# A holographic stage worked off by batch, with query magnitudes inverted on GpSimd

## The chip, the core and the metric

The kernel runs on one core of one Trainium2 chip, as one launch. The metric is the device time of the execution in microseconds, the median of several runs. Beside it there is one profiled execution, whose span runs from the first to the last instruction. In what follows TensorE (PE) does matmuls and transposes, VectorE (DVE), ScalarE (ACT) and GpSimd (POOL) do element work, and SyncE (SP) issues most DMAs.

## What is computed

The reference is a perceiver of two layers on x with 2 batches of 256 tokens of 256 numbers. Each layer has a cross-attention to a context of 4096 tokens, a second attention and a feed-forward part, each added to x. The change lies in the second layer, between its cross-attention and its expert layer, in the "holographic" attention:

```python
    def _L1_attn_ref(x, Wq, bq, Wk, bk, Wv, bv):
        EPS = 1e-08

        def unit_projection(x):
            f = jnp.fft.fft(x)
            f = f / (jnp.abs(f) + EPS)
            return jnp.fft.ifft(f).real

        def bind(a, b):
            return jnp.fft.ifft(jnp.fft.fft(a) * jnp.fft.fft(b)).real

        def unbind(s, a):
            return jnp.fft.ifft(jnp.fft.fft(s) * jnp.conj(jnp.fft.fft(a))).real
        query = unit_projection(jnp.einsum('bsd,ed->bse', x, Wq) + bq)
        keys = unit_projection(jnp.einsum('bsd,ed->bse', x, Wk) + bk)
        values = unit_projection(jnp.einsum('bsd,ed->bse', x, Wv) + bv)
        x_k = bind(keys, values)
        s = jnp.cumsum(x_k, axis=1)
        out = unbind(s, query)
        return out
    ...
    x = x + _L1_xattn_ref(ctx_1024, ctx_1024, _layernorm(x, axis=-1), mask_1x1xSxS2_ik0, L1_xattn_w_out, L1_xattn_b_out)
    x = x + _L1_attn_ref(_layernorm(x, axis=-1), L1_attn_Wq, L1_attn_bq, L1_attn_Wk, L1_attn_bk, L1_attn_Wv, L1_attn_bv)
    x = x + _L1_ffn_ref(_layernorm(x, axis=-1), L1_ffn_sim_matrix, L1_ffn_gates, L1_ffn_q_proj, L1_ffn_k_proj, L1_ffn_v_proj, L1_ffn_o_proj)
```

Queries, keys and values are projections of the normalized x whose every frequency is divided by its magnitude plus 1e-8. Keys and values are multiplied frequency by frequency, summed up along the tokens, and multiplied by the conjugate of the queries.

## The kernel before, in words

Tokens lie on the 128 partitions: 4 token tiles (NT), two to a batch, so that x is a tile of 128 x 4 x 256. A program with a scheduler (the order of each engine's instructions is the scheduler's, except where `keep_in_program_order` fixes it) writes the stages one behind the other.

The second layer's cross-attention (`few_keys` or `any_mask`, one of two branches of the program) leaves its result in `xn`. Behind the branch the tokens are turned by `transpose_tokens`: TensorE transposes into two PSUM tiles, one for each half (k) of the 256 features and all four token tiles, and `evac` copies them to `xnT`, one by VectorE (L44) and one by ScalarE (L46). The output projection (L1515) takes 16 matmul records, and VectorE adds each token tile to x (L1518). Then `layernorm_T(es1, "e")` takes the statistics of all four token tiles (L119, L120), one root of 128 x 4 on ScalarE (L134), its reciprocal (L137), the normalized `xn` (L147), the transposes (L163) and the two copies to `xnT`.

The discrete Fourier transform is folded into the projections (`wq` holds weight times transform, `BD` and `pick` the bias), so `spectrum(j, b)` gives the spectrum of query, key or value (j = 0, 1, 2) of batch b directly: real parts of the frequencies 0 to 128 (NR = 129) and imaginary parts of 1 to 127, two token tiles side by side in one PSUM tile `pf`. From there:

- `keys_values(b, fk, fv)` copies the key spectrum to `ks` and squares both on ScalarE, multiplies the two spectra on VectorE (`product_real`, `product_imag`), takes the magnitudes (`magnitudes`: squares added, root on ScalarE), adds 1e-8 (L1590), multiplies the two magnitudes (L1592), takes the reciprocal on VectorE (L1593), and scales the product `xk` with it (L1594, L1595). The small operations that can be on either engine (`eng`) run on VectorE for batch 0 and on GpSimd for batch 1.
- `query_magnitudes` squares on ScalarE (L1600), adds and adds 1e-8 on GpSimd (L1602); `query_units` takes the reciprocal (L1607) and scales the query spectrum (L1608, L1609) on VectorE.
- `running_sum(b)` sums `xk` along the tokens with three matmuls by `upper` and `ones` (L1614 to L1616). The sum does not go on from one batch to the next.
- `back(b, pc, qn)` multiplies by the conjugate of the queries on VectorE (tile `z`), transposes (L1628), copies (L1630), transforms back (L1634), adds to x (L1639) and takes the statistics for the next layer normalization.

The order in which these are called is:

```python
        kv0 = spectrum(1, 0), spectrum(2, 0)
        keys_values(0, *kv0)
        kv1 = spectrum(1, 1), spectrum(2, 1)
        q0_ = spectrum(0, 0)
        mag0 = query_magnitudes(q0_)
        keys_values(1, *kv1)
        pc0 = running_sum(0)
        q1_ = spectrum(0, 1)
        mag1 = query_magnitudes(q1_)
        qn0 = query_units(q0_, mag0)
        ...
        pc1 = running_sum(1)
        back(0, pc0, qn0)
        qn1 = query_units(q1_, mag1)
        ...
        back(1, pc1, qn1)
```

The expert layer follows: `normalized(b)`, `turned(b)` (L1711, L1714), `expert_weights(b)`, and the projections L1755 in an order that is fixed. TensorE's part of it starts once batch 1 has been through `back`.

Of the kernel before, what the change touches and what calls it, by code (L numbers as in the profile page):

```python
# [9 lines left out]
F32 = mybir.dt.float32  # L10
# [3 lines left out]
ALU = mybir.AluOpType  # L14
# [3 lines left out]
P = 128  # L18
# [8 lines left out]
def tile_perceiver(ctx: ExitStack, tc: tile.TileContext, t):  # L27
    nc = tc.nc

    def pool(es, name, bufs, space=None):  # L30
        kw = {} if space is None else {"space": space}
        return es.enter_context(tc.tile_pool(name=name, bufs=bufs, **kw))
# [84 lines left out]
    def layernorm_stats(mv, sm, tt):  # L117
        st = sm.tile([P, 6], F32, name="st", bufs=2)
        nc.vector.bn_stats(st, x[:, tt, :])  # L119
        nc.vector.bn_aggr(mv[:, tt, :], st)  # L120
# [1384 lines left out]
    with cmp.Else():  # L1505
        any_mask()

    with ExitStack() as es:
        p_s = pool(es, "xo_t", 2, PSUM)
        p_e = pool(es, "xo", 4, PSUM)  # L1510
        transpose_tokens(p_s, xnT, ao)
        for tt in range(NT):
            po = p_e.tile([P, D], F32, name="pe")
            for k in range(2):
                nc.tensor.matmul(  # L1515
                    po, lhsT=xnT[:, k, tt * P : (tt + 1) * P], rhs=wo[:, k, :], start=(k == 0), stop=(k == 1)
                )
            nc.vector.tensor_add(x[:, tt, :], po, x[:, tt, :])  # L1518

    xa.close()  # L1520
    until_xattn.close()
# [6 lines left out]
    with ExitStack() as es:  # L1528
        wk = pool(es, "ha", 1)
        wk2 = pool(es, "ha2", 2)  # L1530
        oproj = wl.tile([P, 8, D], F32, name="oproj")
        nc.sync.dma_start(oproj, t["L1_ffn_o_proj"].rearrange("e d c -> (e d) c").rearrange("(j p) c -> p j c", p=P))

        with ExitStack() as es1:
            layernorm_T(es1, "e")
        ps = pool(es, "ha_p", 6, PSUM)
        ps2 = pool(es, "ha_c", 2, PSUM)
        NR = D // 2 + 1

        def spectrum(j, b):  # L1540

            pf = ps.tile([P, 2, D], F32, name="pf")
            for tb in range(2):
                tt = 2 * b + tb
                for k in range(2):
                    nc.tensor.matmul(  # L1546
                        pf[:, tb, :], lhsT=xnT[:, k, tt * P : (tt + 1) * P], rhs=wq[:, j, k, :],
                        start=(k == 0), stop=False,
                    )
                nc.tensor.matmul(pf[:, tb, :], lhsT=pick[:, j, :], rhs=BD, start=False, stop=True)  # L1550
            return pf

        def magnitudes(eng, sq, tag):

            n = sq.shape[1]
            eng.tensor_tensor(sq[:, :, 1 : NR - 1], sq[:, :, 1 : NR - 1], sq[:, :, NR:D], ALU.add)
            mag = wk2.tile([P, n, NR], F32, name=f"mag{tag}")
            nc.scalar.activation(mag, sq[:, :, 0:NR], AF.Sqrt)
            return mag

        def product_real(out, tmp, a, b_, conj):

            nc.vector.tensor_mul(out[:, :, 0:NR], a[:, :, 0:NR], b_[:, :, 0:NR])
            nc.vector.tensor_mul(tmp, a[:, :, NR:D], b_[:, :, NR:D])
            orr = out[:, :, 1 : NR - 1]
            nc.vector.tensor_tensor(orr, orr, tmp, ALU.add if conj else ALU.subtract)

        def product_imag(out, tmp, a, b_, conj):
            oi = out[:, :, NR:D]
            nc.vector.tensor_mul(oi, a[:, :, NR:D], b_[:, :, 1 : NR - 1])  # L1570
            nc.vector.tensor_mul(tmp, a[:, :, 1 : NR - 1], b_[:, :, NR:D])
            nc.vector.tensor_tensor(oi, oi, tmp, ALU.subtract if conj else ALU.add)

        xks = {}

        def keys_values(b, fk, fv):

            eng = nc.gpsimd if b else nc.vector
            ks = wk2.tile([P, 2, D], F32, name="ks")
            nc.scalar.copy(ks, fk)  # L1580
            sq = wk2.tile([P, 4, D], F32, name="sqkv")
            nc.scalar.activation(sq[:, 0:2, :], fk, AF.Square)
            nc.scalar.activation(sq[:, 2:4, :], fv, AF.Square)
            xk = wk2.tile([P, 2, D], F32, name="xk")
            tmp = wk2.tile([P, 2, NR - 2], F32, name="tmp")
            product_real(xk, tmp, fv, ks, False)
            mag = magnitudes(eng, sq, "kv")
            tmp = wk2.tile([P, 2, NR - 2], F32, name="tmp")
            product_imag(xk, tmp, fv, ks, False)
            eng.tensor_scalar_add(mag, mag, 1e-8)  # L1590
            den = mag[:, 0:2, :]
            eng.tensor_tensor(den, den, mag[:, 2:4, :], ALU.mult)  # L1592
            nc.vector.reciprocal(den, den)  # L1593
            nc.vector.tensor_mul(xk[:, :, 0:NR], xk[:, :, 0:NR], den)  # L1594
            nc.vector.tensor_mul(xk[:, :, NR:D], xk[:, :, NR:D], den[:, :, 1 : NR - 1])  # L1595
            xks[b] = xk

        def query_magnitudes(fq):
            sq = wk2.tile([P, 2, D], F32, name="sqq")
            nc.scalar.activation(sq, fq, AF.Square)  # L1600
            mag = magnitudes(nc.gpsimd, sq, "q")
            nc.gpsimd.tensor_scalar_add(mag, mag, 1e-8)  # L1602
            return mag

        def query_units(fq, mag):
            qn = wk2.tile([P, 2, D], F32, name="qn")
            nc.vector.reciprocal(mag, mag)  # L1607
            nc.vector.tensor_mul(qn[:, :, 0:NR], fq[:, :, 0:NR], mag)  # L1608
            nc.vector.tensor_mul(qn[:, :, NR:D], fq[:, :, NR:D], mag[:, :, 1 : NR - 1])  # L1609
            return qn  # L1610

        def running_sum(b):
            pc = ps2.tile([P, 2, D], F32, name="pc")
            nc.tensor.matmul(pc[:, 0, :], lhsT=upper, rhs=xks[b][:, 0, :], start=True, stop=True)  # L1614
            nc.tensor.matmul(pc[:, 1, :], lhsT=ones, rhs=xks[b][:, 0, :], start=True, stop=False)
            nc.tensor.matmul(pc[:, 1, :], lhsT=upper, rhs=xks[b][:, 1, :], start=False, stop=True)  # L1616
            return pc

        def back(b, pc, qn):
            z = wk2.tile([P, 2, D], F32, name="z")  # L1620
            tmp = wk2.tile([P, 2, NR - 2], F32, name="tmp")
            product_real(z, tmp, pc, qn, True)
            tmp = wk2.tile([P, 2, NR - 2], F32, name="tmp")
            product_imag(z, tmp, pc, qn, True)
            pt = ps.tile([P, 2, S], F32, name="pf")
            for k in range(2):
                for tb in range(2):
                    nc.tensor.transpose(pt[:, k, tb * P : (tb + 1) * P], z[:, tb, k * P : (k + 1) * P], ident)  # L1628
            zT = wk2.tile([P, 2, S], F32, name="zT")
            nc.scalar.copy(zT, pt)  # L1630
            po = ps.tile([P, 2, D], F32, name="pf")
            for tb in range(2):
                for k in range(2):
                    nc.tensor.matmul(  # L1634
                        po[:, tb, :], lhsT=zT[:, k, tb * P : (tb + 1) * P], rhs=idft[:, k, :],
                        start=(k == 0), stop=(k == 1),
                    )
            xb = x[:, 2 * b : 2 * b + 2, :]
            nc.vector.tensor_add(xb, po, xb)  # L1639
            for tt in (2 * b, 2 * b + 1):  # L1640
                layernorm_stats(mvf, wk, tt)

        kv0 = spectrum(1, 0), spectrum(2, 0)
        keys_values(0, *kv0)
        kv1 = spectrum(1, 1), spectrum(2, 1)
        q0_ = spectrum(0, 0)
        mag0 = query_magnitudes(q0_)
        keys_values(1, *kv1)
        pc0 = running_sum(0)
        q1_ = spectrum(0, 1)  # L1650
        mag1 = query_magnitudes(q1_)
        qn0 = query_units(q0_, mag0)

        sims = wl.tile([P, 2, 16], F32, name="sims")
        nc.vector.tensor_mul(sims, sim, sim)
        pc1 = running_sum(1)
        back(0, pc0, qn0)
        qn1 = query_units(q1_, mag1)
        pg = ps.tile([P, 2, D], F32, name="pf")
        for k in range(2):  # L1660
            nc.tensor.matmul(pg[:, 0, 0:16], lhsT=ones, rhs=sims[:, k, :], start=(k == 0), stop=(k == 1))
        rs = wl.tile([P, 16], F32, name="rs")
        nc.scalar.activation(rs, pg[:, 0, 0:16], AF.Sqrt)
        back(1, pc1, qn1)
        nc.vector.tensor_scalar_max(rs, rs, 1e-12)
        nc.vector.reciprocal(rs, rs)
        nc.vector.tensor_mul(sims, sim, rs.unsqueeze(1).to_broadcast([P, 2, 16]))
# [285 lines left out]
```

## Time and profile before

| | |
|---|---|
| median of 3 runs | 585.91 us (582.93 to 587.59) |
| the profiled execution | 581.55 us, of it 579.5 us span |
| TensorE busy | 519.3 us (90%), mean granted clock 0.941 |
| VectorE, ScalarE, GpSimd busy | 259.9, 184.0, 110.0 us |
| output projection, first matmul | 464.52 us |
| first matmul of the spectra | 474.70 us |
| batch 0, then batch 1 added to x (L1639) | 504.32 and 508.48 us |

Times within the span are counted from its start. The stage that the change touches is thus the stretch from some 457 to 509 us of 579.5. The times of the rows are start and duration of instructions; an idle time in brackets is that of the engine just before the instruction, with what ended it.

### The profile page before, as it was taken

The numbers are of one execution on the slowest core, as the hardware profiler recorded it, in microseconds if no ns is written. First come the engines' busy times: TensorE is split into PE (matmuls) and PEld (weight loads), VectorE is DVE, ScalarE is ACT, GpSimd is POOL, SyncE is SP. The second block draws the span as 40 slices with busy tenths as digits, with TensorE's granted clock in tenths as the row PEclk, the third lists the DMA queues.
The fourth block names the chain that finished last, engine by engine and source line by source line (L and its number), as shares of the span: only waits on it lengthen the run. The fifth ranks groups of instructions, "written<-read, shape, count | busy, mean of one in ns | idle before, by whom it ended". The sixth has DMA issues, their size and how long they took to land.

```text
span 579.5 us, 8233 instructions
## 1 busy us (share of the span) xinstructions
PE 519.3 (90%) x3083; PEld 341.6 (59%) x3083; DVE 259.9 (45%) x571; ACT 184.0 (32%) x386; POOL 110.0 (19%) x168
## 2 busy tenths in 40 slices
PE   3999999999896979999994889999999568689997
PEld 3888888883554656666662345444444356444466
DVE  4022241025465531212126757777771047767473
ACT  2211111152565202221222146666666304120110
POOL 8610100105540021100015000000000004016830
PEclk9999999999898799999998679999999779589999
DMA  8999987920002357977822000000000200002301
GB/s 300 327 309 269 276 248 194 164 45 1 1 2 69 115 189 250 298 266 257 303 84 84 1 2 2 2 1 1 3 1 1 78 1 1 1 0 62 86 1 37
DMA packets 53505, 62.73 MB, mean 108 GB/s; under 512 B 16180, under 2 KB 44188, under 8 KB 53452
## 3 DMA queue, kind: packets, MB, share of 16 engines
q1 hardware_dynamic: 45172, 51.76, 30.4%
q10 hardware_dynamic: 6504, 6.18, 3.9%
q0 software_dynamic: 1776, 4.12, 2.2%
q8 instruction: 28, 0.46, 0.3%
q14 instruction: 25, 0.20, 0.1%
HBM read 58.98 MB, written 3.07 MB: 107 GB/s over the span
## 4 chain that ended last, share of the span: by engine, by line
PE 52%; DVE 4%; issue 3%; ACT 2%; POOL 1%; DVEq 0%; SPq 0%; ACTq 0%
PE pe L1020 8%; PE pp L1755 7%; PE pav L1101 6%; PE pm L1003 6%; PE py L732 5%; PE ga L707 4%; PE ua L707 3%; PE pa L1854 2%; PE gb L707 2%; PE pT L721 2%; PE pf L1546 2%; DVE mx L1009 1%; PE pf L1634 1%; ACT e L1027 1%; PE pe L1515 1%
## 5 line engine op out<-in xcount | busy, mean ns | idle before, releaser
L1009 DVE TENSOR_REDUCE mx<-pm 128x2 f32<-128x1024 f32 x64 | 77.9, 1223 | 31.7 <-PE pm L1003 31.5
L1027 ACT ACTIVATE e<-pe 128x512 f32<-128x512 f32 x128 | 72.7, 597 | 43.9 <-PE pe L1020 38.5
L1020 PE MATMUL pe<-qe,both 32*128 32x256 f32 x512 | 76.3, 412 | 2.0 <-DVE mx L1009 1.4
L1003 PE MATMUL pm<-both 32*128 32x512 f32 x256 | 74.4, 710 | 0.9 <-DVE both L990 0.9
L1020 PEld LDWEIGHTS pe<-qe,both 32*128 32x128 f32 x512 | 45.9, 190 | 32.7 <-SPq L1084 24.5
L394 PE MATMUL ph<-xnT,ct 128*128 128x256 f32 x256 | 61.9, 387 | 1.5 <-ACT xnT L46 1.5
L368 PE MATMUL acc<-cn,g 128*128 128x256 f32 x256 | 60.6, 380 | 0.4 <-ACT g L399 0.4
L394 PEld LDWEIGHTS ph<-xnT,ct 128*128 128x128 f32 x256 | 49.6, 195 | 8.7 <-ACT xnT L46 1.9
L368 PEld LDWEIGHTS acc<-cn,g 128*128 128x128 f32 x256 | 48.5, 190 | 8.0 <-ACT g L399 1.2
L399 ACT ACTIVATE g<-ph 128x512 f32<-128x512 f32 x32 | 19.1, 597 | 91.9 <-PE ph L394 63.7
L1755 PE MATMUL pp<-proj,xnT 128*128 128x512 f32 x96 | 44.7, 615 | 0.0
L1101 PE MATMUL pav<-e,both 128*32 128x256 f32 x512 | 40.5, 391 | 0.0
L732 PE MATMUL py<-wd,hT 128*128 128x256 f32 x156 | 38.6, 389 | 1.4 <-ACT hT L723 1.4
L732 PEld LDWEIGHTS py<-wd,hT 128*128 128x128 f32 x156 | 27.9, 189 | 10.5 <-issue 5.6
L331 DVE TENSOR_SCALAR is<-mi 128x512 f32<-128x512 int32 x16 | 6.8, 426 | 58.2 <-DMA mi<-in_maskT 58.2
L1770 POOL TENSOR_TENSOR pw<-pw 128x512 f32<-128x512 f32 (+2 forms) x30 | 25.0, 832 | 38.3 <-DVE pw L1760 36.7
L1755 PEld LDWEIGHTS pp<-proj,xnT 128*128 128x128 f32 x96 | 18.1, 196 | 20.1 <-issue 20.1
L1677 POOL MEMSET causal<- 128x512 f32 x1 | 0.5, 524 | 131.5 <-PE pav L1101 131.5
L1003 PEld LDWEIGHTS pm<-both 32*128 32x128 f32 x256 | 20.2, 203 | 3.7 <-issue 1.7
L1101 PEld LDWEIGHTS pav<-e,both 128*32 128x32 f32 x512 | 10.4, 108 | 20.2 <-issue 19.9
L565 ACT ACTIVATE pr<-sc,mx 128x256 f32<-128x256 f32 x32 | 14.8, 474 | 20.9 <-DVE mx L561 20.9
L738 POOL DMA_INDIRECT xg<-xnd,slot_token x9 | 8.6, 958 | 67.3 <-PE px L747 45.7
(388 smaller groups left out, 724.6 us busy)
## 6 DMA issues: line engine op xcount, KB each, us to landing
ct<-in_ctxT SPq DMA_DIRECT2D x8, 1024.0 KB, 10.4
cn<-in_ctx SPq DMA_DIRECT2D x8, 1024.0 KB, 11.9
wg<-in_L_ffn_we_gate SPq DMA_DIRECT2D x9, 688.0 KB, 5.5
wu<-in_L_ffn_we_up SPq DMA_DIRECT2D x9, 688.0 KB, 6.4
wd<-in_L_ffn_we_down SPq DMA_DIRECT2D x9, 640.0 KB, 4.7
mi<-in_maskT ACTq DMA_DIRECT2D x16, 256.0 KB, 5.6
both<-in_ctxT SPq DMA_DIRECT2D x8, 256.0 KB, 9.4
R<-rwd SPq DMA_DIRECT2D x4, 512.0 KB, 6.1
```

Source lines behind the costliest of these rows:

```text
L368: nc.tensor.matmul(acc[e][qb], lhsT=g[:, j, qb * P : (qb + 1) * P], rhs=cn[:, fc % 8 + j, :], start=(fc + j == 0), stop=(fc + j == NKC - 1),)
L394: nc.tensor.matmul(ph[:, j, :], lhsT=ct[:, k, f0 : f0 + P], rhs=xnT[:, k, e * D : (e + 1) * D], start=(k == 0), stop=(k == 1),)
L399: gelu = nc.scalar.activation(g, ph, AF.Gelu_apprx_tanh)
L707: nc.tensor.matmul(out[:, 0:n], lhsT=xT[k], rhs=m[:, k, f0 : f0 + n], start=(k == 0), stop=(k == 1))
L732: nc.tensor.matmul(py, lhsT=hT[0:m, c, :], rhs=w[2][0:m, c, :], start=(c == 0), stop=(c == NC6 - 1))
L1003: put(nc.tensor.matmul(pm[:, j, :], lhsT=qm[32 * g : 32 * g + 32, u, qb * P : (qb + 1) * P], rhs=kq[32 * g : 32 * g + 32, u, c * 512 : (c ...
L1009: nc.vector.tensor_reduce(mxs[u][:, qb, c, 2 * pair : 2 * pair + 2], pm, axis=AX.X, op=ALU.max)
L1020: return put(nc.tensor.matmul(pe[:, j * S : (j + 1) * S], lhsT=kq[32 * g : 32 * g + 32, u, n * P : (n + 1) * P], rhs=qes[u][32 * g : 32 * ...
L1027: nc.scalar.activation(e.rearrange("p j q -> p (j q)"), pe, AF.Exp, scale=1.0 / 16.0)
L1101: put(nc.tensor.matmul(pa[32 * g : 32 * g + 32, :], lhsT=VF[:, b * FEW + n, 17 * h : 17 * h + 32], rhs=es_of.pop((v, g, n)), start=(n == 0 ...
L1755: in_turn(nc.tensor.matmul(pp[:, hf * 512 : (hf + 1) * 512], lhsT=xnT[:, k, tt * P : (tt + 1) * P], rhs=proj[:, j, k, hf * 512 : (hf + 1) ...
L1770: nc.gpsimd.tensor_tensor(pw[:, 0:n], pw[:, 0:n], pw[:, n : 2 * n], ALU.add)
```

## The change

The output projection's stage now goes by batch. `transpose_batch` writes both halves of one batch into one PSUM tile, with one copy for each batch: ScalarE copies batch 0 and VectorE batch 1 ahead of the projection, ScalarE both ahead of the spectra. The statistics of the layer normalization are taken right behind each addition to x. Root, reciprocal and normalization are done for each batch by itself, and `layernorm_T` is not called here any more.

In the holographic stage the queries of a batch come behind its keys and values in the program: query spectrum 0 ahead of the spectra of batch 1. The query spectrum is copied to SBUF by ScalarE (`qs`). The 1e-8 is added by ScalarE (Identity with the bias `tiny`), for keys, values and queries alike. `query_units` raises the magnitudes to the power of -1 on GpSimd (the exponent is a tile `minus` of 128 x 2 x 129) and GpSimd multiplies `qs` by them in two products. In `keys_values` the magnitudes are multiplied ahead of the imaginary part of the product; the reciprocal of keys and values stays on VectorE.

```diff
--- before.py
+++ after.py
@@ -1505,10 +1505,29 @@
     with cmp.Else():
         any_mask()
 
+    mve = cst.tile([P, NT, 2], F32, name="mve")
+    rstde = cst.tile([P, NT], F32, name="rstde")
+    tiny = cst.tile([P, 1], F32, name="tiny")
+    nc.gpsimd.memset(tiny, 1e-8)
+    minus = cst.tile([P, 2, 129], F32, name="minus")
+    nc.gpsimd.memset(minus, -1.0)
+
+    def transpose_batch(pt, b, copy):
+
+        ps = pt.tile([P, 2, S], F32, name="ps_t")
+        for k in range(2):
+            for tb in range(2):
+                nc.tensor.transpose(
+                    ps[:, k, tb * P : (tb + 1) * P], xn[:, 2 * b + tb, k * P : (k + 1) * P], ident
+                )
+        copy(xnT[:, :, b * S : (b + 1) * S], ps)
+
     with ExitStack() as es:
+        xo = pool(es, "xo_s", 2)
         p_s = pool(es, "xo_t", 2, PSUM)
         p_e = pool(es, "xo", 4, PSUM)
-        transpose_tokens(p_s, xnT, ao)
+        for b in range(B):
+            transpose_batch(p_s, b, nc.vector.tensor_copy if b else nc.scalar.copy)
         for tt in range(NT):
             po = p_e.tile([P, D], F32, name="pe")
             for k in range(2):
@@ -1516,6 +1535,17 @@
                     po, lhsT=xnT[:, k, tt * P : (tt + 1) * P], rhs=wo[:, k, :], start=(k == 0), stop=(k == 1)
                 )
             nc.vector.tensor_add(x[:, tt, :], po, x[:, tt, :])
+            layernorm_stats(mve, xo, tt)
+        for b in range(B):
+            two = slice(2 * b, 2 * b + 2)
+            nc.scalar.activation(rstde[:, two], mve[:, two, 1], AF.Sqrt, bias=eps)
+            nc.vector.reciprocal(rstde[:, two], rstde[:, two])
+            for tt in (2 * b, 2 * b + 1):
+                nc.vector.tensor_scalar(
+                    xn[:, tt, :], x[:, tt, :], mve[:, tt, 0:1], rstde[:, tt : tt + 1],
+                    op0=ALU.subtract, op1=ALU.mult,
+                )
+            transpose_batch(p_s, b, nc.scalar.copy)
 
     xa.close()
     until_xattn.close()
@@ -1531,8 +1561,6 @@
         oproj = wl.tile([P, 8, D], F32, name="oproj")
         nc.sync.dma_start(oproj, t["L1_ffn_o_proj"].rearrange("e d c -> (e d) c").rearrange("(j p) c -> p j c", p=P))
 
-        with ExitStack() as es1:
-            layernorm_T(es1, "e")
         ps = pool(es, "ha_p", 6, PSUM)
         ps2 = pool(es, "ha_c", 2, PSUM)
         NR = D // 2 + 1
@@ -1556,6 +1584,7 @@
             eng.tensor_tensor(sq[:, :, 1 : NR - 1], sq[:, :, 1 : NR - 1], sq[:, :, NR:D], ALU.add)
             mag = wk2.tile([P, n, NR], F32, name=f"mag{tag}")
             nc.scalar.activation(mag, sq[:, :, 0:NR], AF.Sqrt)
+            nc.scalar.activation(mag, mag, AF.Identity, bias=tiny)
             return mag
 
         def product_real(out, tmp, a, b_, conj):
@@ -1565,11 +1594,11 @@
             orr = out[:, :, 1 : NR - 1]
             nc.vector.tensor_tensor(orr, orr, tmp, ALU.add if conj else ALU.subtract)
 
-        def product_imag(out, tmp, a, b_, conj):
+        def product_imag(out, tmp, a, b_, conj, eng=nc.vector):
             oi = out[:, :, NR:D]
-            nc.vector.tensor_mul(oi, a[:, :, NR:D], b_[:, :, 1 : NR - 1])
-            nc.vector.tensor_mul(tmp, a[:, :, 1 : NR - 1], b_[:, :, NR:D])
-            nc.vector.tensor_tensor(oi, oi, tmp, ALU.subtract if conj else ALU.add)
+            eng.tensor_tensor(oi, a[:, :, NR:D], b_[:, :, 1 : NR - 1], ALU.mult)
+            eng.tensor_tensor(tmp, a[:, :, 1 : NR - 1], b_[:, :, NR:D], ALU.mult)
+            eng.tensor_tensor(oi, oi, tmp, ALU.subtract if conj else ALU.add)
 
         xks = {}
 
@@ -1583,31 +1612,29 @@
             nc.scalar.activation(sq[:, 2:4, :], fv, AF.Square)
             xk = wk2.tile([P, 2, D], F32, name="xk")
             tmp = wk2.tile([P, 2, NR - 2], F32, name="tmp")
+            mag = magnitudes(eng, sq, "kv")
             product_real(xk, tmp, fv, ks, False)
-            mag = magnitudes(eng, sq, "kv")
+            den = mag[:, 0:2, :]
+            eng.tensor_tensor(den, den, mag[:, 2:4, :], ALU.mult)
             tmp = wk2.tile([P, 2, NR - 2], F32, name="tmp")
             product_imag(xk, tmp, fv, ks, False)
-            eng.tensor_scalar_add(mag, mag, 1e-8)
-            den = mag[:, 0:2, :]
-            eng.tensor_tensor(den, den, mag[:, 2:4, :], ALU.mult)
             nc.vector.reciprocal(den, den)
             nc.vector.tensor_mul(xk[:, :, 0:NR], xk[:, :, 0:NR], den)
             nc.vector.tensor_mul(xk[:, :, NR:D], xk[:, :, NR:D], den[:, :, 1 : NR - 1])
             xks[b] = xk
 
         def query_magnitudes(fq):
+            qs = wk2.tile([P, 2, D], F32, name="qs")
+            nc.scalar.copy(qs, fq)
             sq = wk2.tile([P, 2, D], F32, name="sqq")
             nc.scalar.activation(sq, fq, AF.Square)
-            mag = magnitudes(nc.gpsimd, sq, "q")
-            nc.gpsimd.tensor_scalar_add(mag, mag, 1e-8)
-            return mag
-
-        def query_units(fq, mag):
-            qn = wk2.tile([P, 2, D], F32, name="qn")
-            nc.vector.reciprocal(mag, mag)
-            nc.vector.tensor_mul(qn[:, :, 0:NR], fq[:, :, 0:NR], mag)
-            nc.vector.tensor_mul(qn[:, :, NR:D], fq[:, :, NR:D], mag[:, :, 1 : NR - 1])
-            return qn
+            return qs, magnitudes(nc.gpsimd, sq, "q")
+
+        def query_units(qs, mag):
+            nc.gpsimd.tensor_tensor(mag, mag, minus, ALU.pow)
+            nc.gpsimd.tensor_tensor(qs[:, :, 0:NR], qs[:, :, 0:NR], mag, ALU.mult)
+            nc.gpsimd.tensor_tensor(qs[:, :, NR:D], qs[:, :, NR:D], mag[:, :, 1 : NR - 1], ALU.mult)
+            return qs
 
         def running_sum(b):
             pc = ps2.tile([P, 2, D], F32, name="pc")
@@ -1641,21 +1668,20 @@
                 layernorm_stats(mvf, wk, tt)
 
         kv0 = spectrum(1, 0), spectrum(2, 0)
+        q0 = spectrum(0, 0)
         keys_values(0, *kv0)
+        mag0 = query_magnitudes(q0)
         kv1 = spectrum(1, 1), spectrum(2, 1)
-        q0_ = spectrum(0, 0)
-        mag0 = query_magnitudes(q0_)
+        qn0 = query_units(*mag0)
         keys_values(1, *kv1)
         pc0 = running_sum(0)
-        q1_ = spectrum(0, 1)
-        mag1 = query_magnitudes(q1_)
-        qn0 = query_units(q0_, mag0)
+        mag1 = query_magnitudes(spectrum(0, 1))
 
         sims = wl.tile([P, 2, 16], F32, name="sims")
         nc.vector.tensor_mul(sims, sim, sim)
         pc1 = running_sum(1)
         back(0, pc0, qn0)
-        qn1 = query_units(q1_, mag1)
+        qn1 = query_units(*mag1)
         pg = ps.tile([P, 2, D], F32, name="pf")
         for k in range(2):
             nc.tensor.matmul(pg[:, 0, 0:16], lhsT=ones, rhs=sims[:, k, :], start=(k == 0), stop=(k == 1))
```

## The prediction

> **What bounds the kernel now.** I read the page's head first, for the engines and the profiled span, then the chain of work that ended last inside the stretch that the change touches, then that stretch in order of time. The chain from the end of the masked cross-attention to the first expert projection is this (start, duration, engine, tile, line):
>
> ```profile
> 456.73 5.90 issue
> 463.78 0.70 DVE xnT L44
> 464.52 3.70 PE pe L1515 x8
> ...
> 471.85 0.19 DVE rstd L137
> ...
> 474.03 0.59 ACT xnT L46
> ...
> 485.13 1.27 POOL sqkv L1556
> ...
> 489.63 1.76 DVE magkv L1593
> ...
> 492.86 1.74 DVE magq L1607 x2
> ...
> 506.45 2.01 PE pf L1634 x8
> 508.48 0.69 DVE x L1639
> ```
>
> The reader sees two parts. Up to 474.7 us the chain is a strict relay: copy, projection, statistics, root, normalization, transpose, copy. From 481 to 501 it is VectorE, with a detour through GpSimd and ScalarE for the magnitudes of batch 1. At 508.48 the second batch's result is added to x, and TensorE goes on to the expert projections, which it alone bounds. So the change is worth the shift of that 508.48. The profiled execution took 581.55 us, 579.5 of them span; the runs' median is 585.91, 4.36 above it. I work out the shift on the profiled execution and add it to the median.
>
> The timeline prices the steps (start, duration, engine, line, operation; in brackets the idle time before it):
>
> ```profile
> 463.67 0.19 DVE L1655 TENSOR_TENSOR sims<-sim 128x32 f32<-128x32 f32 x1 [6.71 <-issue]
> ...
> 484.33 0.42 DVE L1592 TENSOR_TENSOR magkv<-magkv 128x258 f32<-128x258 f32 x1
> 484.79 1.77 DVE L1593 RECIPROCAL magkv<-magkv 128x258 f32<-128x258 f32 x1
> 485.13 1.26 POOL L1556 TENSOR_TENSOR sqkv<-sqkv 128x508 f32<-128x508 f32 x1 [28.86 <-ACT sqkv L1583]
> 486.43 0.63 ACT L1558 ACTIVATE magkv<-sqkv 128x516 f32<-128x516 f32 x1 [1.38 <-POOL sqkv L1556]
> 488.96 0.64 POOL L1592 TENSOR_TENSOR magkv<-magkv 128x258 f32<-128x258 f32 x1
> 490.31 0.42 ACT L1558 ACTIVATE magq<-sqq 128x258 f32<-128x258 f32 x1 [2.76 <-POOL sqq L1556]
> 490.64 0.58 ACT L1600 ACTIVATE sqq<-pf 128x512 f32<-128x512 f32 x1
> 490.81 0.87 POOL L1602 TENSOR_SCALAR magq<-magq 128x258 f32<-128x258 f32 x1 [0.54 <-ACT magq L1558]
> 492.79 3.38 DVE L1607 RECIPROCAL magq<-magq 128x258 f32<-128x258 f32 x2
> ```
>
> GpSimd does a plain product of 258 elements in 0.64 us. VectorE needs 0.42 for one and 1.77 for a reciprocal. No row holds a power.
>
> **The front of the stage.** Now the first tokens' product waits for VectorE, whose first instruction after the branch comes at 463.67, while TensorE's transposes were done at 461.53 and ScalarE copied from 461.57. After the change ScalarE copies batch 0 (0.59), so the projection starts at 462.2, 2.3 earlier. VectorE's copy of batch 1 (463.8 to 464.5) hides behind batch 0's two token tiles, whose sums now come 2.1 and 3.7 us after the start, so until 465.9; without that cover it would cost up to the 2.3. Statistics end at 471.14 - 2.3 = 468.8. Batch 0's root is taken while batch 1's statistics run, which removes the 0.70 that VectorE waits at L137; the second reciprocal gives 0.2 back. Batch 0's copy hides behind batch 1's transposes, where today 0.6 of copy stands open; the rest of the sum is gaps of some 0.2. The spectra start at 471.0 in place of 474.7, a gain of 3.7. TensorE's order there is otherwise unchanged. On ScalarE two roots of 128x2 replace one of 128x4, 0.3 each, inside waits. The two new fills on GpSimd stand near the start of the program, far from any wait, at 0.3 like fills of that size. No DMA is added, moved or passed.
>
> **The query chain.** The third spectrum, now the queries of batch 0, is done 7.7 after the start, at 478.7. ScalarE first does the root of the keys and values and the added Identity pass with the bias (0.64 each, to 479.4), then a copy and a square (0.58 each, 480.5). GpSimd adds the squares (0.75, 481.3), ScalarE takes the root (0.42), copies batch 1's keys, which stand in front (0.58), and adds the bias (0.42). GpSimd can start the first power at 482.9. Call its price P. Behind it on GpSimd's queue stand its two products (0.65 each), then batch 1's whole key and value work, then the second query. In that order:
> - query 0 ready: 482.9 + P + 1.35 = 484.25 + P;
> - batch 1's squares (1.26 on GpSimd), root and bias (0.64 each), gaps: 486.95 + P; the product of magnitudes (0.64), VectorE's reciprocal (1.76) and two products: xk of batch 1 at 490.2 + P, against 492.86 today;
> - query 1's copy and square on ScalarE (1.2), squares added (0.75), root and bias (0.85 and gaps): second power at 489.95 + P, ready at 491.3 + 2P;
> - six VectorE products for z (0.33 each, the first under GpSimd's last product): 492.8 + 2P.
>
> Batch 0 occupies TensorE until 497.9 + P (z at 491.8 + P, transposes 1.0, copy 0.6, inverse spectrum 3.78 as now, the small product 0.67). The rest, from z's transposes to the add to x, took 504.79 to 508.48, 3.7. So x of batch 1 comes at 501.6 + P while P is under 5.1, a shift of P - 6.9, and at 496.5 + 2P beyond, a shift of 2P - 12.0. Beyond P = 8 TensorE stands idle for 3 us or more ahead of it, and its clock has fallen by then:
>
> ```profile
> 498.00:505.00 7.00, 5.84 (x17) 4.33 (x18) 4.17 (x12) 0.60 (x2) 0.00 (x0) 0.50 0.00 0
> 505.00:512.00 7.00, 4.82 (x25) 3.53 (x25) 4.41 (x22) 3.09 (x8) 0.00 (x0) 0.96 0.00 0
> ```
>
> This is the table by stage; the last column but two is the granted clock, 0.50 and then 0.96. The eight matmuls of the inverse spectrum took 3.78 us at the first and 1.99 at the second, so add 1.8: a shift of 2P - 10.2.
>
> VectorE sheds two query reciprocals (3.4), four products (1.6) and small adds. That counts for nothing once it waits for GpSimd: the 6.9 in the first formula already holds it. In VectorE's queue the first product of z 0 stands ahead of batch 1's reciprocal; it waits for 484.25 + P, and the reciprocal's own input comes 3.3 later, so nothing is lost there.
>
> **The price of P.** The lower end is one plain pass, 0.64. A power with a full-size exponent tile is no plain pass: I assume that it is worked out as a logarithm, a product and an exponential, each logarithm and exponential some ten multiply-adds. That is an assumption about arithmetic, not a row. At 20 passes of the 0.64 row it costs 12.8; at 40, if each waits for the one ahead of it, 25.6, my upper end. Between the two ends stands VectorE's reciprocal at 4.2 plain passes (1.77 by 0.42), which on GpSimd would be 2.7; but that is a single iterated division. The power is nearer to the two polynomials, so I take 12.8. Shift: 2 x 12.8 - 10.2 = +15.4, so 597 on the profiled execution's base and 601.3 on the median's.
>
> The Trainium skill's GPSIMD Engine Reference (section 3.1) says that a loop body of three or more operations for an element runs at about three operations a cycle. By that, an estimate: 20 multiply-adds in perhaps 60 operations are 20 cycles at 1.2 GHz, 4.3 us for 258 elements, and the time would be 583. No row here shows such a body. The same page (section 4.1) advises against elementwise work on GpSimd.
>
> **The rivals.** (1) The power is cheap, at most about a pass and a half, because it is done like any other operation: place, GpSimd's two powers. For it: GpSimd is busy 3.9 of the 9 us from 489 to 498, and VectorE, which it relieves, 8.4. Against it: even the simpler division costs 4.2 passes on VectorE. It decides below P = 1; at 0.64 the shift is -6.3, 579.6 us. (2) A middling power, P from 1 to 8, where the front's 3.7 and VectorE's relief pay for it; at 2.7 the shift is -4.2, 581.7; break-even is P = 6. (3) The front gains nothing because ScalarE's first instruction after the branch comes as late as VectorE's, the branch's code being laid out anew: every time rises by up to 3.7, to 605 at my P and 585.4 at 2.7; it shifts, but decides only near break-even. That the change does not do what it says is ruled out by the order of the built instructions: queries stand where it says, GpSimd holds the two powers, and VectorE has two reciprocals of this stage, not four.
>
> **How the numbers follow.** Within 1% is about what a measurement of this kernel can tell from no change. More than 1% slower needs P over 8: 0.70, of which 0.13 lies beyond 25.6. Within 1% (rival 2): 0.20. More than 1% faster (rival 1): 0.10. Rival 3 has 0.15 in any of them and moves little chance across. The likeliest case has its own range of 592 to 627, P from 8 to 25.6. The full range reaches down to rival 1, 580, and leaves out the dearest powers.
>
> **What would show it.** In the profile after: the first matmul of the projection about 0.7 us after the transposes end and spectra 3.7 earlier; GpSimd's two powers as its longest instructions, some 13 us each; TensorE and VectorE idle on GpSimd between about 489 and 516. A power row under 2 us makes the forecast wrong at the root; one of 13 with no such idle time would mean that I have misread the queue.

## The result and the profile after

The changed kernel takes 656.45 us in the median of four runs, and the kernel before 585.02 beside it, 71 us more. The ratios here and below, with 95% intervals, are of fast executions alone, so they can differ a little from the quotient of two medians (here 1.128, 1.1236 to 1.1324, against 1.122). A gain in us that stands beside a ratio is worked out from the ratio. The forecast was slower, at 601.3 us with a range up to 627. The profiled execution took 656.98 us, 655.1 of them span.

Two lines of the page of the kernel after, the busy time of the engines and the share of each engine in the chain of work that ended last:

```profile
PE 521.6 (80%) x3083; PEld 343.3 (52%) x3083; DVE 254.5 (39%) x564; ACT 188.1 (29%) x394; POOL 193.1 (29%) x173
...
PE 45%; POOL 14%; DVE 3%; ACT 3%; issue 2%; DVEq 0%; SPq 0%; ACTq 0%
```

GpSimd was busy for 110.0 us before and is for 193.1 now, and its share of the chain went from 1% to 14%. The chain through the stage (start, duration, engine, tile, line) shows where:

```profile
470.60 0.59 ACT xnT L1523
...
471.23 1.54 PE pf L1574 x4
...
480.91 0.73 POOL sqq L1584
...
483.04 41.75 POOL magq L1634
...
526.18 1.40 POOL sqkv L1584
...
530.04 0.73 POOL sqq L1584
...
531.84 41.78 POOL magq L1634
...
574.37 0.64 POOL qs L1636
...
578.33 3.80 PE pf L1661 x8
582.15 0.70 DVE x L1666
```

L1634 is the power. Two of them, 41.75 us each, stand one behind the other in a chain that otherwise goes as it was worked out. The waits of the kernel after (engine, tile, line, what it waited for, us in total, times, longest) say who stood still meanwhile:

```profile
DVE z L1592 <- POOL qs L1635: 79.8, 2, 40.0
PE pc L1641 <- DVE xk L1623: 46.6, 1, 46.6
...
PE pf L1655 <- DVE z L1595: 36.4, 1, 36.4
```

VectorE waits twice for a query that GpSimd has not finished, and TensorE behind VectorE.

Since the stage begins at another time in every execution, I measure it from the first matmul record of the transposes ahead of the output projection to batch 1's add to x. The transposes in the timeline before, then after:

```profile
459.59 1.94 PE L163 MATMUL ps_t<-ident,xn 128*128 128x128 f32 x8 [3.20 <-issue]
...
460.04 1.94 PE L1520 MATMUL ps_t<-ident,xn 128*128 128x128 f32 x8 [3.05 <-issue]
```

The add comes at 508.48 before and 582.15 after, so the stage takes **48.9 us before, 122.1 after**, 73.2 more. The rest of the 75.6 between the two spans is 0.45 ahead of the stage and 1.9 behind it. Behind it TensorE runs at a lower clock than before: its next transposes and the eight small matmuls after them took 1.12 and 1.89 us where they had taken 0.66 and 1.06, and from 582 to 588 us the granted clock was 0.50 (0.96 from 505 to 512 us before).

### The profile page after: what moved, and what is told of

Read it like the earlier page. It is cut to its first block, busy times and chain, and to the rows that moved or that the text cites. A ratio compares the mean times of both kernels' runs of the same rounds, so it can differ in the third digit from the quotient of the medians.

```text
span 655.1 us, 8241 instructions
## 1 busy us (share of the span) xinstructions
PE 521.6 (80%) x3083; PEld 343.3 (52%) x3083; DVE 254.5 (39%) x564; ACT 188.1 (29%) x394; POOL 193.1 (29%) x173
## 4 chain that ended last, share of the span: by engine, by line
PE 45%; POOL 14%; DVE 3%; ACT 3%; issue 2%; DVEq 0%; SPq 0%; ACTq 0%
POOL magq L1634 13%; PE pe L1020 7%; PE pp L1781 7%; PE pav L1101 5%; PE pm L1003 5%; PE py L732 5%; PE ga L707 3%; PE ua L707 3%; PE pa L1880 2%; PE gb L707 2%; PE pT L721 1%; DVE mx L1009 1%; PE pf L1574 1%; ACT e L1027 1%; PE pf L1661 1%
## 5 line engine op out<-in xcount | busy, mean ns | idle before, releaser
L1634 POOL TENSOR_TENSOR magq<-magq,minus 128x258 f32<-128x258 f32 x2 | 83.5, 41756 | 2.5 <-ACT magq L1587 2.5
L1641 PE MATMUL pc<-xk,upper 128*128 128x256 f32 x4 | 1.9, 566 | 46.6 <-DVE xk L1623 46.6
L1655 PE MATMUL pf<-ident,z 128*128 128x128 f32 x8 | 2.4, 430 | 36.5 <-DVE z L1595 36.4
```

The costliest lines, as they stand in the source:

```text
L1634: nc.gpsimd.tensor_tensor(mag, mag, minus, ALU.pow)
```

## The experiments

### The power replaced by a plain product

```diff
-            nc.gpsimd.tensor_tensor(mag, mag, minus, ALU.pow)
+            nc.gpsimd.tensor_tensor(mag, mag, minus, ALU.mult)
```

> The power is replaced by a product with the same tile of -1, so that the magnitudes are not inverted; all else, and the order of every instruction, is that of the changed kernel. Theory A (the two powers at 41.75 us are the whole loss, and the rest of the change gains what the prediction worked out): GpSimd's instruction takes 0.64 us, the shift against the kernel before is P - 6.9 = -6.3 us, about -1.1%, and batch 1 is added to x at about 502 us of the span. Rival B (the queue costs too: keys and values of batch 1 stand behind the queries on GpSimd, and ScalarE has six more instructions): not faster than before, batch 1 added at 508 us or later.

Measured: 576.37 us against 581.85, ratio 0.9913 (0.9879 to 0.9946), so 5.1 us less; the stage takes 42.0 us (461.71 to 503.75), 6.9 less than before. This kernel leaves out the inversion, so it only prices the rest of the change. Its GpSimd rows from the timeline:

```profile
484.72 0.80 POOL L1634 TENSOR_TENSOR magq<-magq,minus 128x258 f32<-128x258 f32 x1 [1.41 <-ACT magq L1587]
...
492.59 0.87 POOL L1634 TENSOR_TENSOR magq<-magq,minus 128x258 f32<-128x258 f32 x1 [1.07 <-ACT magq L1587]
```

The instruction order is that of the changed kernel, and so are all other instructions. So the 80 us between the two stages (122.1 and 42.0) come with the power alone, not with the queue, the longer ScalarE list or the order by batch: theory A. With the first of these rows in place of P, the first formula gives -6.1, near the 6.9 less, but in part by luck: the formula has batch 0's inverse spectrum at 3.78 us, and it took 1.99 here, on the path, which is worth 1.8.

### Half the power

```diff
-            nc.gpsimd.tensor_tensor(mag, mag, minus, ALU.pow)
+            nc.gpsimd.tensor_tensor(mag[:, 0, :], mag[:, 0, :], minus[:, 0, :], ALU.pow)
```

> The changed kernel with the power taken of one of the two token tiles only (129 numbers, the other tile's magnitudes are left as they are); the order of every instruction is that of the changed kernel. Theory A (the price goes with the number of elements, 0.162 us each): 20.9 us an instruction, shift 2 x 20.9 - 10.2 = +31.6 us, 617 us. Rival C (a fixed price, as from loading the code of the power or a first call): 41 us again, 656 us; if only the first of the two is dear, the second is short.

Measured: 613.56 us (one run, the kernel before at 581.85), 31.7 more; the stage 80.7 us (457.77 to 538.49), 31.8 more.

```profile
480.60 21.12 POOL L1634 TENSOR_TENSOR magq<-magq,minus 128x129 f32<-128x129 f32 x1 [1.41 <-ACT magq L1587]
...
508.79 21.16 POOL L1634 TENSOR_TENSOR magq<-magq,minus 128x129 f32<-128x129 f32 x1 [1.07 <-ACT magq L1587]
```

Half the elements cost half, both times; a first call or loaded code (rival C) is out. The 2P - 10.2 of the prediction holds at a second price: 31.6 with the 20.9 expected, 32.1 with the 21.14 measured, and the stage grew by 31.8.

### The price of a power by itself

```diff
+    for n in (16, 64, 256):
+        res = cst.tile([P, n], F32, name=f"res{n}")
+        nc.gpsimd.tensor_tensor(res, grown[:, 0:n], lower[:, 0:n], ALU.pow)
...
+    nc.gpsimd.tensor_tensor(rone, ones[:, 0:64], lower[:, 0:64], ALU.pow)
...
+    nc.gpsimd.tensor_tensor(rhalf, grown[:, 0:64], half, ALU.pow)
...
+    nc.gpsimd.tensor_tensor(rts[0:32], grown[0:32, 0:64], lower[0:32, 0:64], ALU.pow)
```

Here `grown` counts from 1 to 256, `lower` is -1 and `half` 0.5; the lines left out make the tiles.

> The kernel before with six powers more on GpSimd, early in the program, that nothing uses; only their rows are read, not the kernel's time. Theory A (the same work for every element, whatever the values): 0.162 us for each element of the free dimension, so 2.6 us for 16, 10.4 for 64, 41.5 for 256; 10.4 too for 64 elements of base 1, for 64 with the exponent 0.5 in place of -1, and for 64 on 32 partitions in place of 128. Rival D (an iteration or branch that depends on the data): base 1 or exponent 0.5 differ by over 10%. Rival C (a fixed part, or code that is loaded for the first power): the first, of 16 elements, takes well over 2.6 us.

Measured, in the groups of instructions (line, engine, operation, tiles, shape, count, busy us, mean ns, idle before):

```profile
L971 POOL TENSOR_TENSOR res<-grown,lower 128x256 f32<-128x256 f32 x1 | 41.2, 41230 | 0.0
L971 POOL TENSOR_TENSOR res<-grown,lower 128x64 f32<-128x64 f32 x1 | 10.5, 10542 | 0.0
L973 POOL TENSOR_TENSOR rone<-ones,lower 128x64 f32<-128x64 f32 x1 | 10.5, 10532 | 0.0
L975 POOL TENSOR_TENSOR rhalf<-grown,half 128x64 f32<-128x64 f32 x1 | 10.5, 10532 | 0.0
L977 POOL TENSOR_TENSOR rts<-grown,lower 32x64 f32<-32x64 f32 x1 | 10.5, 10532 | 0.0
...
L971 POOL TENSOR_TENSOR res<-grown,lower 128x16 f32<-128x16 f32 x1 | 3.0, 2951 | 0.1
```

From 64 to 256 elements it is 30.69 us for 192, 0.160 us each, and some 0.3 fixed. Base 1, the exponent 0.5 and a quarter of the partitions change nothing: rivals C and D fall. The first power, of 16 elements, has 0.4 fixed by the same slope, so it pays next to nothing for being the first. Per element of the free dimension a power is 64 plain products (0.64 us for 258, 2.5 ns each).

### One power instead of two

```diff
+            if power:
+                nc.gpsimd.tensor_tensor(mag, mag, minus, ALU.pow)
+            else:
+                nc.vector.reciprocal(mag, mag)
...
-        qn1 = query_units(*mag1)
+        qn1 = query_units(*mag1, power=False)
```

> The power for batch 0's queries alone; batch 1's magnitudes are inverted by VectorE's reciprocal. Theory A (two powers one behind the other, each in full on the path): one power leaves the branch P - 6.9 of the sum, +34.9 us, some 617 us; the transposes of the stage's start to batch 1's add take 84 to 86 us (48.9 before, 122.1 after). Rival E (the powers overlap with other work, so that the first is largely hidden): below 610 us.

Measured: 614.15 us (one run), 32.5 more than the kernel before's 581.64; the stage 81.5 us (459.67 to 541.14). The changed kernel's stage is 40.6 longer than this one. The second power less the reciprocal in its place is 40.0 of that; batch 1's inverse spectrum, 3.78 us there and 1.99 here, adds 1.8, and 1.2 go the other way: the reciprocal, for one, stands behind batch 0's products on VectorE, at 532.09 though its input was done at 530.48. Against the 84 to 86 expected the stage is 2.5 below the lower end; 1.8 of that is batch 0's inverse spectrum, which ran in 1.99 us and not in the 3.78 that I had put in. Rival E falls: beside the kernel with both reciprocals on VectorE (below, 42.3 us) this one, with a power for the first of them, takes 39.2 longer, where power less reciprocal is 40.0, so next to nothing hides the first power.

### The front alone, twice

The layer normalization by batch in the kernel before; its holographic stage is left as it was.

> Only the front by batch (copies, statistics, root and normalization of each batch) in the kernel before; the holographic stage is that of before. Theory A: the spectra start 3.5 to 3.7 us earlier and the whole gain reaches the end: -3.6 us, -0.6%. Rival B (the gain is lost on the way, as VectorE or the code after the branch is late): the spectra start earlier by under 1.5 us, or batch 1 is added to x no earlier than at 507.5 us; within 0.2%.

Measured: 577.56 us against 581.85, ratio 0.9926 (0.9892 to 0.996). The stage takes 45.0 us (461.97 to 506.98), 3.9 less than before. It was run again in the last group, on another chip:

> The front by batch alone once more, beside the two others on the same chip, to compare the three against one kernel before. Theory A (45.0 us from the stage's start to batch 1's add, 48.9 before): 0.993 of the kernel before; the two others 0.988 to 0.991. Rival B (the differences between these orders lie below what the runs can tell): all three between 0.990 and 0.997.

Measured: 579.60 against 581.94, ratio 0.9959 (0.9921 to 0.9997), stage 44.6 us. Both intervals lie below 1 and share 0.9921 to 0.996, so the front gains, about half a percent. Theory A holds for the stage, where the profiles show 3.9 and 4.3; the runs can't tell its last microsecond. Of the three kernels that were run side by side on that chip, the two others (0.997 and 0.9897, below) do not both fall where either expectation has them.

### The reciprocal back on VectorE, and who bounds the stage then

```diff
-            nc.gpsimd.tensor_tensor(mag, mag, minus, ALU.pow)
+            nc.vector.reciprocal(mag, mag)
```

> The power is replaced by VectorE's reciprocal of the same 258 numbers; the products stay on GpSimd, and the front and the order by batch stay. Theory A: two reciprocals of 1.76 us come back onto VectorE, one of them under waits; the shift is -3 to -6 us against the kernel before (-0.5% to -1%). Rival B (VectorE's queue bounds the stage whatever the order): within 0.3% of the kernel before, because the 3.5 us are back in front of z.

Measured: 578.87 against 581.85, ratio 0.9952 (0.9916 to 0.9989); the stage 42.3 us. The runs lie just below the expected gain and the one profile just above it; the interval reaches into rival B's 0.3%, so it is the stage that speaks against B. Why the runs give 2.8 us where the stage shows 6.6 less stays open. The profiled execution itself reached the stage 3.9 us later than that of the kernel before (463.50 against 459.59), and the profiles of this case differ by up to 6 us there (457.77 to 463.60), ahead of the stage; one profile each can't tell whether that is chance.

Then batch 0's way back was put ahead of batch 1's keys and values, first by itself and then with `eng = nc.vector` for batch 1's small operations too:

```diff
+        pc0 = running_sum(0)
+        back(0, pc0, qn0)
         keys_values(1, *kv1)
-        pc0 = running_sum(0)
         mag1 = query_magnitudes(spectrum(0, 1))
...
         pc1 = running_sum(1)
-        back(0, pc0, qn0)
```

> The reciprocals on VectorE as in the second kernel of the first group, and batch 0's way back (its z, transposes and inverse spectrum) put ahead of batch 1's keys and values in the program. Theory A (behind the reciprocals TensorE's order bounds the end: the inverse spectrum of batch 0 stands ahead of batch 1's z): start of the stage to batch 1's add 40 to 41.5 us in place of 42.3, and 1% below the kernel before. Rival B (VectorE's queue bounds: six operations of batch 0 now stand ahead of batch 1's keys): 42.3 us or more.

> As the kernel ahead of this one in the group, with the squares' addition and the magnitudes' product of batch 1 on VectorE too, so that GpSimd keeps only the queries' work. Theory A (GpSimd's longer operations, 1.26 and 0.64 us in place of 0.68 and 0.42, lie on batch 1's path): 0.5 to 1 us less than that kernel. Rival B (VectorE's queue bounds): 0.5 to 1 us more.

Measured: 583.76 us, ratio 1.0059 (1.0026 to 1.0092), stage 47.5 us; and 583.89, ratio 1.0022 (0.9989 to 1.0054), stage 48.4. Theory A fell for both; between the two, where the stages differ by 0.9, the runs tell no difference. The timeline of the first of the two shows a queue that I had not followed:

```profile
489.70 3.78 PE L1661 MATMUL pf<-idft,zT 128*128 128x256 f32 x8 [0.68 <-ACT zT L1657]
...
493.27 1.19 PE L1574 MATMUL pf<-wq,xnT 128*128 128x256 f32 x4
493.52 0.69 DVE L1666 TENSOR_TENSOR x<-pf,x 128x512 f32<-128x512 f32 x1 [2.29 <-PE pf L1661]
494.13 0.42 DVE L1622 TENSOR_TENSOR xk<-xk,magkv 128x258 f32<-128x258 f32 x1
...
498.49 1.77 DVE L1634 RECIPROCAL magq<-magq 128x258 f32<-128x258 f32 x1 [0.41 <-ACT magq L1587]
```

Batch 1's query spectrum now stands behind batch 0's inverse spectrum on TensorE, so its reciprocal comes at 498.49, and VectorE's scaling of `xk` stands behind batch 0's add to x, which waits for TensorE. To test that, the query spectrum was put ahead of the way back:

```diff
         pc0 = running_sum(0)
+        q1 = spectrum(0, 1)
         back(0, pc0, qn0)
         keys_values(1, *kv1)
-        mag1 = query_magnitudes(spectrum(0, 1))
+        mag1 = query_magnitudes(q1)
```

> Batch 0's way back ahead of batch 1's keys and values, with batch 1's query spectrum ahead of it on TensorE. Theory A (what batch 0's early way back lost, 47.5 us in place of 42.3, was the query spectrum of batch 1 queued behind batch 0's inverse spectrum on TensorE, at 493.3 us): 42 to 43.6 us. Rival B (it was VectorE's queue, with batch 0's six operations and its add to x ahead of batch 1's): 46 us or more.

Measured: 578.71 against 581.94, ratio 0.997 (0.993 to 1.0009); the stage 43.2 us (463.60 to 506.75). That gives back 4.4 of the 5.2 us lost: the query spectrum's place on TensorE was the larger part. The stage is still 0.8 longer than with the way back last (one profile of each); batch 1's inverse spectrum took 3.58 us here and 1.99 there.

### A version ahead of both

The reciprocals on VectorE as above, the change's order, and batch 1's squares and magnitude product on VectorE too:

```diff
-            eng = nc.gpsimd if b else nc.vector
+            eng = nc.vector
```

> The changed kernel with the reciprocals on VectorE and the squares' addition and magnitudes' product of batch 1 on VectorE, so that GpSimd keeps only the queries' work; batch 0's way back stays where the change has it. Theory A (with the reciprocal's price gone, GpSimd's 1.26 and 0.64 us lie on batch 1's path): start of the stage to batch 1's add 41 to 42.3 us (42.3 with GpSimd). Rival B (VectorE's queue bounds, and gets 1.1 us more): 43 us or more. Either way about 1% below the kernel before if the front's 3.9 us hold.

Measured: 575.59 against 581.94, ratio 0.9897 (0.9864 to 0.9929); the stage 41.4 us:

```profile
489.26 1.76 DVE L1634 RECIPROCAL magq<-magq 128x258 f32<-128x258 f32 x1
...
499.76 0.69 DVE L1666 TENSOR_TENSOR x<-pf,x 128x512 f32<-128x512 f32 x1 [0.40 <-PE pf L1661]
```

Theory A by the stage, 0.9 less than with GpSimd, and 1% ahead of the kernel before. With one profile of each this is argued rather than shown: batch 0's inverse spectrum took 3.51 us here and 3.78 there, and the interval of the ratio overlaps that of the version with GpSimd (0.9916 to 0.9989). It has the lowest ratio of the versions that were run with the computation whole; the front alone, at 0.9926 (0.9892 to 0.996), is not clearly behind it.

## Why the prediction was right and wrong

**The step that failed is the price of P.** I put 12.8 us, 20 plain passes, with 25.6 as the upper end; it is 41.75, 65 passes. The upper end was no bound. It rested on how many steps I supposed a power to have and on a row of another operation as the price of each. No row of the trace holds a logarithm, an exponential or anything like them on GpSimd, so the rows bounded P from below alone. The chance that I gave to all powers dearer than 25.6 was 0.13, and the range left them out. The Trainium skill's GPSIMD Engine Reference, section 3.1, with its three operations a cycle, led to an estimate of 4.3 us. The measured row is almost ten times that; whether the power runs more operations or runs them more slowly, no run here tells.

**The rest of the sum held.** Put 41.75 for P into the prediction's last formula: 2 x 41.75 - 10.2 = 73.3. The stage became 73.2 longer. Step by step, with the 0.45 by which the stage began later:
- spectra: 471.0 predicted, 471.23 measured; 3.9 earlier within the stage, where 3.7 was worked out. Two errors cancel in that: the projection began 3.2 earlier and not 2.3, because ScalarE copied batch 0 (461.16) while batch 1's transposes still ran (until 461.98), and from there to the spectra 0.7 was gained and not 1.4. VectorE's first instruction after the branch came at 463.69, ScalarE's copy at 461.16, so rival 3 did not happen;
- first power: 482.9 predicted, 483.04 measured; query 0 ready at 526.0 and 526.18; the second power at 531.7 and 531.84; batch 1's add at 581.8 and 582.15;
- the clock: the eight matmuls of batch 1's inverse spectrum took 3.78 us as put in, at a granted clock of 0.50 in this table by stage (the last column but two). Batch 0's took 1.99 and not the 3.78 worked out, off the chain here:

```profile
576.00:582.00 6.00, 5.02 (x12) 3.10 (x12) 3.69 (x15) 0.97 (x3) 0.00 (x0) 0.50 0.00 0
```

What the sum left out is the stretch behind the stage, which became 1.9 longer; the prediction took the shift of batch 1's add for the whole change.

**The rivals.** A cheap power (1) is out, but its own price is shown: with the plain product the kernel gains 5.1 us in the runs and 6.9 in the stage, where 6.3 was given and 1.8 came from the faster inverse spectrum. The middling power (2) is out too. So what the change does around the power is worth about 1%, and the two powers take 80 us of stage from it (122.1 against 42.0).

## What to carry to other kernels

An operation that no row shows has no upper bound from the other rows; time it alone in a spare place of the queue before it is put on a path, with two sizes to part the fixed price from the slope. An engine that is idle is no free place for it: here GpSimd was idle for most of the stage, and two powers on its queue, 83.5 us together, put 80 us onto the end. A formula with the unknown price left in it was worth more than the forecast: it gave the growth of the stage within half a microsecond once the price was known, at two prices (41.75 and 21.14 us).

## What the runs showed of the hardware that was not expected

A power on GpSimd (tensor with tensor) costs 0.160 us for each element of the free dimension and some 0.3 fixed, the same for 32 partitions as for 128 and for the bases (1, and 1 to 64) and exponents (-1, 0.5) tried; VectorE's reciprocal of the same 258 numbers takes 1.76 us against 41.75. And ScalarE's Identity with a bias tile takes longer than its root without one: 0.73 against 0.63 us for 516 elements, 0.51 against 0.42 for 258. That lies in the bias tile rather than in the function, as two roots of the same size in the kernel after show, one with the tile `eps` and one without:

```profile
578.59 0.30 ACT L1720 ACTIVATE rstd<-mvf,eps 128x2 f32<-128x2 f32 x1 [0.31 <-DVE mvf L120]
...
578.79 0.19 ACT L1722 ACTIVATE rn<-mvf 128x2 f32<-128x2 f32 x1
```
